# Layer 0 of a two-layer gated attention kernel: tables and mask made in steps 5 to 9, maxima over partitions by turning, first loads in pieces, slots cleared beside attention

## The chip, the core and the metric

The kernel runs on one core of a Trainium2 chip. The metric is the device time in microseconds, the median of several runs. The core has a matrix engine (PE), a vector engine (DVE), an activation engine (ACT), a general engine (POOL) and an engine that mostly issues transfers (SP). Each works through its own queue of instructions in order and waits on semaphores for the others. 16 DMA engines carry the transfers, and all of this kernel's plain transfers but the row scatters are issued from SP's queue.

## The reference, cut to what matters

```python
# x: (4, 512, 512); ctx: (4, 512, 512)
x = x + tanh(g_xattn[0]) * L0_xattn(layernorm(x), ctx)   # fp8-like rounding of both, then x @ ctx^T
x = x + tanh(g_ffn[0])   * L0_ffn(layernorm(x), w1, w2)  # 1.58-bit weights, int8-like rows, gelu twice
x = x + tanh(g_xattn[1]) * L1_xattn(layernorm(x), ctx, ctx, mask, ...)  # 16 heads, ALiBi, softmax
x = x + tanh(g_ffn[1])   * L1_ffn(layernorm(x), ...)     # 8 experts, top 2, plus a shared expert

def quant_dequant_weight_128x128(w):          # used on ctx in L0_xattn
    amax = max(|block of 128 x 128|)          # a maximum over 128 partitions too
    safe = maximum(amax, 1e-6)
    return float(fp8(block * (448 / safe))) * (safe / 448)
```

Layer 0 needs, of the context, one maximum for each block of 128 x 128. Layer 1's attention needs tables (ALiBi slopes and mask rows in bf16) that are added to the scores by small matmuls, and a column form of the mask. Layer 1's experts need a buffer in DRAM, `slots`, that is cleared before rows are scattered into it.

## The kernel before, in words

The 2048 rows of x are 16 tiles of 128 rows; four tiles share one of four context batches. Layer 0 is a software pipeline of steps, `step(s)` for s from -7 to 17. Step s works on several tiles at once: `cross_rows` and `cross_product` for tiles s+7 and s+6 (layer norm, rounding in blocks, product with the context, added to x), `row_stats`, `row_norm`, `row_quant`, `row_ready` for tiles s+1 to s+6 (layer norm, int16 rows, a transpose by DMA, conversion to bf16), `hidden` for tile s (the first feed-forward product and two gelus), `hidden_scales` and `hidden_quant` for tile s-1 (maximum, scale, int16 rows, a transpose by DMA in `turn`), and `down` for tile s-2 (the second product). So the feed-forward of tile 0 begins in step 0; steps -7 to -1 fill the pipeline, and beside them the weights w1 and w2 are loaded, summed (`weight_sum`), averaged (`weight_mean`) and rounded (`weight_round`).

`cross_context(b)` prepares batch b of the context: keys and values for layer 1 by matmuls with wk and wv, the blocks' maxima (line 681 within partitions, line 683 over the partitions by `partition_all_reduce` on POOL), and then, for each of four chunks, a scaling by `up` (line 692), the rounding in four DVE instructions (`fp8_round`, lines 136 to 141) and a scaling back on ACT (line 699).

The program's order is not the engines' order. A recording layer takes all the instructions and a planner places them on each engine by their costs and by what they need; only those given to `keep_in_program_order` (in layer 0 the ACT instructions under `pin`) stay in the order written. The order is fixed when the program is built: at run time each engine goes through its queue in order, and an instruction whose input is late holds up all behind it.

At the start, `load_batch(0)` brings 1024 KB of context in one transfer and `load_rows(0)` 1024 KB of x in one (lines 568 and 572); then come the gates, wk, wv, and the mask's column form, which lines 589 to 604 turn into `mk` and `mbias`. `tables(tmp)` (lines 160 to 219) makes the layer 1 tables: `pick` (line 189, four POOL copies of 128x128), `by_query` (line 191, two POOL copies of 128x2048), and on DVE and ACT the ALiBi rows (lines 197 to 210); line 212 loads the mask's rows and line 217 copies them into `by_key` in four transfers, which wait on SP for DVE. The planner put nearly all of this at the head of the queues.

Eight semaphores are handed round the transfers of SP's queue: a transfer waits until the one eight before it has landed.

`clear_slots` (line 1028) writes zeros from `row_tables`' tail to `slots`, 771 KB for each of 13 transfers; its calls stand in the attention's loop, but it waits for nothing there, and the planner put all 13 on SP between 55 and 104 us.

Attention is a loop over 16 groups, each of four units. For group n the maxima are made in turn n, they are turned and copied into `by_query` rows (line 340) in turn n+1, and the weights are made in turn n+2; `keys` (line 238) fetches a group's keys two turns ahead. Two turns of it stand within the last steps of layer 0. After attention come the shared expert, the router, the scatter into `slots`, and 36 expert tiles.

Of the kernel before, what the change touches and what calls it, by code (L numbers as in the profile page):

```python
# [10 lines left out]
F32 = mybir.dt.float32  # L11
# [37 lines left out]
def flamingo_kernel(  # L49
# [110 lines left out]
    def tables(pool):  # L160

        place_i = pool.tile([P, 1], I32, name="place_i")
# [24 lines left out]
        for b in range(B):  # L187
            nc.vector.tensor_tensor(own[b], own[b], no_mask, ALU.add)
            nc.gpsimd.tensor_copy(pick[:, b, :], own[b].to_broadcast([P, P]))
        for n in range(2):  # L190
            nc.gpsimd.tensor_copy(
                by_query[n], no_mask.unsqueeze(2).to_broadcast([P, NG, S])
            )
# [9 lines left out]
        split3(ali3, ali, ali_rest)  # L203
        nc.vector.tensor_scalar(ali, ali3[:, 0, :], part[0], late, ALU.mult, ALU.add)
# [9 lines left out]
        nc.vector.tensor_scalar(mrow, mrow8, -1.0, 2.0**100, ALU.add, ALU.mult)  # L214
        for i in range(HPG):
# [18 lines left out]
    def keys(b, g):  # L234

        k4 = qk.tile([P, S], F32, tag="k4", name=f"k4_{b}_{g}", bufs=5)
        for i in range(HPG):
            nc.sync.dma_start(
                out=k4[32 * i : 32 * i + 32, :], in_=kT[32 * g : 32 * g + 32, b, :]
            )  # L240
        state["k4", b, g] = k4
# [306 lines left out]
    with ExitStack() as l0:  # L548
# [9 lines left out]
        with ExitStack() as ph:  # L558
# [7 lines left out]
            def load_batch(b):  # L566
                c = cpool.tile([P, DC, S], F32, tag="ctx", name=f"ctx_{b}")
                nc.sync.dma_start(out=c, in_=ctxT[b].rearrange("(c p) n -> p c n", p=P))
                state["ctx", b] = c

            def load_rows(b):
                nc.sync.dma_start(
                    out=x_sb[:, b * TB : (b + 1) * TB, :], in_=x_t[:, b * TB : (b + 1) * TB, :]
                )
# [10 lines left out]


            mk8 = wkv.tile([P, B, TB], U8, name="mk8")
            nc.sync.dma_start(out=mk8, in_=mask_col)
            nc.vector.tensor_copy(mk, mk8)
            cnt_ps = acc("cnt_ps")  # L590
            nc.tensor.matmul(
                cnt_ps[:, : B * TB],
                lhsT=ones,
                rhs=mk.rearrange("p b c -> p (b c)"),
                start=True,
                stop=True,
            )
            anyk = wkv.tile([P, B], F32, name="anyk")
            nc.vector.tensor_reduce(
                anyk, cnt_ps[:, : B * TB].rearrange("p (b c) -> p b c", b=B), AX.X, ALU.max  # L600
            )
            nc.vector.tensor_scalar_min(anyk, anyk, 1.0)
            for b in range(B):
                nc.vector.tensor_scalar(
# [939 lines left out]
```

## Time and profile before

| What | us |
|---|---|
| Runs, median of 3 (lowest to highest) | 1310.45 (1305.22 to 1312.64) |
| The profiled execution: time, span | 1314.13, 1312.4 |
| Feed-forward of tile 0 starts on PE (line 837) | 113.20 |
| Feed-forward of tile 15 starts on PE | 308.53 |
| Attention's first scores on PE | 320.32 |
| First expert tile's transposes on PE | 993.87 |
| PE busy in the span | 1182.9 (90%) |
| DVE, ACT, POOL busy in the span | 609.9, 512.9, 426.1 |

A row of the time line gives the start in us, the time from the first to the last instruction in us, the engine, the line of the code, the operation, what it writes and reads, the count, and in brackets how long the engine sat idle before it and what released it; `issue` there is time in which nothing that the profile shows was waited for. SPq rows are the issuing of transfers, not the transfers. Instructions on DVE overlap a little, so that ten of 0.68 us follow each other every 0.60 us. A row of the windows gives, for a stretch of the span, each engine's busy time (and the number of instructions), then the granted clock of PE as a share of full speed, the DMA engines' busy share, and GB/s.

### The profile page before, as it was taken

How to read it: one execution, taken by the hardware profiler on the slowest of the kernel's cores; microseconds unless marked ns; L12 is line 12 of the kernel's file. 1: busy time of each engine (PE TensorE's matmuls, PEld its weight loads, DVE VectorE, ACT ScalarE, POOL GpSimd, SP SyncE). 2: the span in 40 equal slices, each digit the busy share in tenths (PEclk: the TensorE clock that was granted, in tenths of full speed). 3: DMA queues.
4: the chain of work that ended last, by engine and by line, in shares of the span. 5: the costliest groups of instructions: out<-in, count | busy, mean ns of one | idle time of the engine just before them, and what ended most of it. 6: DMA issues, size and time to landing. Idle time of an engine off the chain costs nothing. (4 is left out here: it accounts for less than half of the span.)

```text
span 1312.4 us, 14470 instructions
## 1 busy us (share of the span) xinstructions
PE 1182.9 (90%) x5348; PEld 546.2 (42%) x5348; DVE 609.9 (46%) x1135; ACT 512.9 (39%) x711; POOL 426.1 (32%) x417
## 2 busy tenths in 40 slices
PE   3457878888799999999999999999999999999995
PEld 2224433333333333333332555543335555555553
DVE  7699887786656666566663501331122111111110
ACT  2588878876255555444454111100001111111111
POOL 3200100010167876776778301126100111111111
PEclk9679988999999999999999899999999999999998
DMA  6782212343000000000003000017315876888782
GB/s 220 259 288 86 45 36 46 92 101 84 17 10 18 9 18 9 10 18 9 2 1 137 9 0 0 0 43 297 87 64 160 265 214 192 255 257 260 220 252 33
DMA packets 88658, 135.33 MB, mean 103 GB/s; under 512 B 52741, under 2 KB 54025, under 8 KB 84745
## 3 DMA queue, kind: packets, MB, share of 16 engines
q1 hardware_dynamic: 80840, 116.52, 27.9%
q0 software_dynamic: 7744, 17.86, 6.3%
q8 instruction: 43, 0.70, 0.2%
q14 instruction: 31, 0.25, 0.1%
HBM read 113.84 MB, written 32.32 MB: 111 GB/s over the span
## 5 line engine op out<-in xcount | busy, mean ns | idle before, releaser
L418 ACT ACTIVATE ex<-s,mbias,mk 128x1024 f32<-128x1024 f32 x128 | 147.2, 1200 | 140.0 <-PE s L232 140.0
L310 DVE TENSOR_REDUCE nmax<-s 128x2 f32<-128x1024 f32 x128 | 150.4, 1216 | 100.6 <-PE s L232 89.8
L1394 PE MATMUL gue<-w,xT 128*128 128x352 f32 x576 | 176.1, 459 | 0.0
L1430 POOL DMA_INDIRECT out_dram<-ye,row_i x36 | 55.7, 1546 | 323.8 <-ACT ye L1429 219.6
L379 POOL TENSOR_TENSOR part<-part,ex 128x1024 f32<-128x1024 f32 x62 | 144.6, 2352 | 16.5 <-PE sm L232 11.4
L1151 PE MATMUL gu<-xnT_d,w 128*128 128x512 f32 x320 | 143.4, 608 | 0.0
L1394 PEld LDWEIGHTS gue<-w,xT 128*128 128x128 f32 x576 | 109.2, 190 | 70.6 <-issue 16.9
L1414 DVE COPY hT<-tph_e 128x256 f32<-128x256 f32 x36 | 15.3, 424 | 255.2 <-PE tph_e L1412 255.2
L1421 PE MATMUL oe<-w,hT 128*128 128x512 f32 (+1 forms) x216 | 102.4, 609 | 3.8 <-ACT ye L1429 0.6
L1151 PEld LDWEIGHTS gu<-xnT_d,w 128*128 128x128 f32 x320 | 62.3, 195 | 77.9 <-issue 77.9
L883 PE MATMUL ob<-w2q,hqT 128*128 128x512 bf16 x256 | 66.1, 412 | 26.1 <-DVE hqT L815 25.4
L1140 ACT ACTIVATE sg<-gu,sgb 128x512 f32<-128x512 f32 x20 | 13.7, 687 | 177.0 <-PE gu L1151 170.8
L379 POOL TENSOR_TENSOR part<-ex,ex 128x1024 f32<-128x1024 f32 x32 | 75.8, 2390 | 21.2 <-ACT ex L418 21.1
L232 PE MATMUL s<-row_tables 10*128 10x512 bf16 (+1 forms) x512 | 68.1, 385 | 13.3 <-DVE nmax L310 10.5
L1402 ACT ACTIVATE sge<-gue 128x352 f32<-128x352 f32 x36 | 16.7, 463 | 151.5 <-PE gue L1394 151.5
L232 PE MATMUL s<-qT,k 32*128 32x512 f32 x512 | 72.4, 605 | 0.0
L232 PE MATMUL s<-k,qT 32*128 32x512 f32 x512 | 72.0, 601 | 0.0
L738 PE MATMUL oa<-ctx,vTa 128*128 128x512 f32 x128 | 63.4, 642 | 8.2 <-ACT vTa L735 8.2
L232 PE MATMUL av<-ex,kv 128*32 128x512 f32 x512 | 69.9, 610 | 0.4 <-ACT ex L418 0.4
L1141 DVE SCALAR_TENSOR_TENSOR hd<-gu,sub,sg 128x512 f32<-128x512 f32 x20 | 15.0, 751 | 117.3 <-ACT sg L1140 104.4
L232 PE MATMUL q_ps<-xnT,wq_sb 128*128 128x512 f32 (+1 forms) x158 | 69.5, 551 | 0.0
L232 PE MATMUL oc<-wo,attnT 128*128 128x512 f32 (+1 forms) x164 | 66.2, 525 | 0.0
(251 smaller groups left out, 1694.2 us busy)
## 6 DMA issues: line engine op xcount, KB each, us to landing
w<-in_e_w_dram SPq DMA_DIRECT2D x36, 1408.0 KB
w<-in_e_w_dram SPq DMA_DIRECT2D x36, 768.0 KB
slots<-row_tables SPq DMA_DIRECT2D x13, 771.0 KB
xr<-slots SPq DMA_DIRECT2D x36, 256.0 KB
ctx<-in_ctxT_dram SPq DMA_DIRECT2D x4, 1024.0 KB
x_sb<-in_x_dram SPq DMA_DIRECT2D x4, 1024.0 KB
stage<-in_w1T_dram SPq DMA_DIRECT2D x4, 1024.0 KB
stage<-in_w2T_dram SPq DMA_DIRECT2D x4, 1024.0 KB
```

Source lines behind the costliest of these rows:

```text
L232: tc.keep_in_program_order(nc.tensor.matmul(*args, **how))
L310: nc.vector.tensor_reduce(nmax[:, i, 2 * j : 2 * j + 2], sc[j], AX.X, ALU.max, negate=True)
L379: nc.gpsimd.tensor_tensor(part[:, hs, :], old[:, hs, :], ex[:, hs, :], ALU.add)
L418: nc.scalar.activation(ex[:, 2 * j : 2 * j + 2, :], sc[j], AF.Exp, bias=mbias[:, b, kc : kc + 1], scale=mk[:, b, kc : kc + 1],)
L738: nc.tensor.matmul(o_ps[:, 0, :], lhsT=vT[:, dc, :], rhs=cq[:, dc, :], start=dc == 0, stop=dc == DC - 1,)
L883: nc.tensor.matmul(o_ps, lhsT=hqT[:, c, :], rhs=w2q[:, c * D : (c + 1) * D], start=c == 0, stop=c == IC - 1,)
L1151: nc.tensor.matmul(gu[:, m, :], lhsT=w[:, dc, c * P : (c + 1) * P], rhs=xnT[:, dc, b * S : (b + 1) * S], start=dc == 0, stop=dc == DC - 1,)
L1394: nc.tensor.matmul(gu[:, m, :I], lhsT=xT[:, dc, :], rhs=wt[:, dc, :], start=dc == 0, stop=dc == DC - 1,)
L1402: nc.scalar.activation(sg, gu[:, 0, :I], AF.Silu)
L1414: nc.vector.tensor_copy(hT[:, :2, :], tp[:, : 2 * P].rearrange("p (c q) -> p c q", q=P))
L1421: nc.tensor.matmul(o_ps[:, 0, :], lhsT=hT[:ni, c, :], rhs=dw[:ni, c, :], start=c == 0, stop=c == len(ICH) - 1,)
L1430: added = nc.gpsimd.indirect_dma_start(out=out, out_offset=bass.IndirectOffsetOnAxis(ap=row_i[:, j, 0:1].bitcast(I32), axis=0), in_=y, in_ ...
```

## The change

- `cross_context`: the maximum over partitions no longer uses POOL. PE transposes the 16 columns of maxima into PSUM (16 x 128), DVE takes the maximum along the row and spreads it over 128 columns, PE transposes that back, and the floor of 1e-6 is taken from PSUM. For batch 0 the maximum within partitions is taken in four pieces of one chunk each.
- `load_batch(0)` and `load_rows(0)` are four transfers each, of 256 KB.
- `tables` is now a generator of five pieces. `pick` and `by_query` are made on DVE from a bf16 tile of ones: four multiplications of 128x128 and eight of 128x512. One piece is made in each of steps 5 to 9, and the mask's column form (now `key_mask`) in step 6. A piece's DVE instructions are queued behind the last maximum of the hidden rows written so far (`state["peak"]`, line 882 of the changed kernel), and its transfers behind the last transpose (`state["turned"]`); its POOL and ACT instructions are free.
- `clear_slots` is queued on SP behind the last key fetch written so far (`state["fetch"]`).

```diff
 def tables(pool):
...
-            nc.gpsimd.tensor_copy(pick[:, b, :], own[b].to_broadcast([P, P]))
+        yield
+        wide = pool.tile([P, S], BF16, name="wide")
+        nc.gpsimd.memset(wide, 1.0)
+        for b in range(B):
+            nc.vector.tensor_scalar_mul(pick[:, b, :], wide[:, :P], own[b])
         for n in range(2):
-            nc.gpsimd.tensor_copy(
-                by_query[n], no_mask.unsqueeze(2).to_broadcast([P, NG, S])
-            )
+            for g in range(NG):
+                nc.vector.tensor_scalar_mul(by_query[n][:, g, :], wide, no_mask)
+        yield
...
 def load_batch(b):
-                nc.sync.dma_start(out=c, in_=ctxT[b].rearrange("(c p) n -> p c n", p=P))
+                src = ctxT[b].rearrange("(c p) n -> p c n", p=P)
+                for dc in [slice(k, k + 1) for k in range(DC)] if b == 0 else [slice(DC)]:
+                    nc.sync.dma_start(out=c[:, dc, :], in_=src[:, dc, :])
...
 def cross_context(b):
-                nc.vector.tensor_reduce(am, cb, AX.X, ALU.max, apply_absolute_value=True)
+                for ns in [slice(4 * dc, 4 * dc + 4) for dc in range(DC)] if b == 0 else [slice(16)]:
+                    nc.vector.tensor_reduce(
+                        am[:, ns], cb[:, ns, :], AX.X, ALU.max, apply_absolute_value=True
+                    )
+                tp = acc(f"tpm_{b}")
+                nc.tensor.transpose(tp[:16, :P], am, ident)
+                peak = small.tile([16, 1], F32, tag="cpeak", name=f"cpeak_{b}", bufs=2)
+                nc.vector.tensor_reduce(peak, tp[:16, :P], AX.X, ALU.max)
+                wide = small.tile([16, P], F32, tag="cwide", name=f"cwide_{b}", bufs=2)
+                nc.vector.tensor_copy(wide, peak.to_broadcast([16, P]))
+                nc.tensor.transpose(tp[:, P : P + 16], wide, ident[:16, :16])
                 safe = small.tile([P, 16], F32, tag="csafe", name=f"csafe_{b}", bufs=2)
-                nc.gpsimd.partition_all_reduce(safe, am, P, bass_isa.ReduceOp.max)
-                nc.vector.tensor_scalar_max(safe, safe, 1e-6)
+                nc.vector.tensor_scalar_max(safe, tp[:, P : P + 16], 1e-6)
...
-                tables(tmp)
                 load_batch(1)
...
-            for s in range(5, NT - 6):
-                step(s)
+            with tc.tile_pool(name="tmp", bufs=1) as tmp:
+                made = tables(tmp)
+
+                def made_here():
+                    with tc.issue_after(state["peak"]), tc.issue_after(state["turned"]):
+                        go(made)
+                        if s == 6:
+                            key_mask()
+
+                for s in range(5, NT - 6):
+                    step(s, [made_here])
...
-                clear_slots(min(3 * (n - 2), MT), min(3 * (n - 2) + 3, MT))
+                with tc.issue_after(state["fetch"]):
+                    clear_slots(min(3 * (n - 2), MT), min(3 * (n - 2) + 3, MT))
```

`load_rows(0)` is cut in the same way as `load_batch(0)`. The order that the planner gives the changed kernel's instructions is known without running it; where the prediction speaks of the new order, it is that. In it POOL's queue holds no `partition_all_reduce`, SP's holds one clearing of `slots` in layer 0 and twelve in attention, and on DVE the pieces of the tables follow the hidden maximum of tile 4.

## The prediction

> **What bounds the kernel now.** I read the slices first, then the windows by stage, then POOL's and DVE's time lines in the first 115 us, then one steady step.
>
> ```profile
> PE   3457878888799999999999999999999999999995
> DVE  7699887786656666566663501331122111111110
> PEclk9679988999999999999999899999999999999998
> ```
>
> Each digit is 32.8 us. From the twelfth on PE is full: attention and the experts are PE's, and whatever starts them earlier ends them earlier. Before that no engine is full all the time, and DVE comes nearest.
>
> ```profile
> 0.00:6.40 6.40, 0.00 (x0) 0.00 (x0) 0.01 (x1) 1.28 (x1) 1.85 (x14) 1.00 0.62 229
> 40.90:46.70 5.80, 0.00 (x0) 0.00 (x0) 0.26 (x3) 1.47 (x6) 0.46 (x2) 0.50 0.89 306
> 63.20:113.20 50.00, 34.95 (x133) 19.45 (x132) 47.06 (x126) 37.94 (x72) 2.96 (x3) 0.86 0.75 261
> 113.20:187.50 74.30, 59.39 (x226) 28.41 (x225) 66.67 (x165) 63.86 (x105) 7.17 (x8) 0.93 0.16 31
> 187.50:245.00 57.50, 46.43 (x177) 21.09 (x176) 43.94 (x107) 48.78 (x71) 4.29 (x6) 0.91 0.24 47
> 320.30:1312.40 992.10, 956.81 (x4487) 437.20 (x4486) 353.98 (x496) 277.76 (x357) 381.74 (x354) 0.98 0.31 95
> ```
>
> Third busy column: DVE works 47.06 of the 50 us ahead of tile 0's feed-forward (113.20) and 66.67 of the next 74.3. So the start is DVE's, but for two holes, the first load and 40.9 to 46.7. In the last row PE works 956.81 of 992.10: 35 us are idle, and no edit but the slot writes touches this stage.
>
> ```profile
> 16.74 4.18 POOL L191 CAST row_tables<-no_mask 128x2048 bf16<-128x2048 f32 x2
> 27.89 8.93 POOL L126 TENSOR_TENSOR rstd_a<-ve_a,mhalf 128x4 f32<-128x4 f32 x1 [6.96 <-DVE ce L136]
> 46.24 0.39 POOL L683 PARTITION_ALL_REDUCE csafe<-cam  x1 [9.42 <-issue]
> 62.75 0.39 POOL L683 PARTITION_ALL_REDUCE csafe<-cam  x1 [6.11 <-issue]
> ```
>
> The same power on 128x4 takes 1.05 us elsewhere and 8.93 here, and each all-reduce that follows a power has an unexplained 6 to 9 us ahead of it: POOL changes over between the two kinds, and each change costs that. DVE pays:
>
> ```profile
> 6.39 2.29 DVE L681 TENSOR_REDUCE cam<-ctx 128x16 f32<-128x2048 f32 x1 [6.39 <-DMA ctx<-in_ctxT_dram]
> 17.23 1.94 DVE L206 SCALAR_TENSOR_TENSOR ali<-ali,part,ali 128x512 f32<-128x512 bf16 x1
> 46.66 0.62 DVE L684 TENSOR_SCALAR csafe<-csafe 128x16 f32<-128x16 f32 x1 [5.54 <-POOL csafe L683]
> 63.17 0.17 DVE L684 TENSOR_SCALAR csafe<-csafe 128x16 f32<-128x16 f32 x1 [3.78 <-POOL csafe L683]
> ```
>
> 5.54 and 3.78 us stand still at the head of DVE's queue. L206 takes 1.94 beside POOL's L191 and 0.84 without it; the csafe at 19.10 takes 1.86 against 0.17.
>
> **The start, part by part.** Removed from DVE ahead of tile 0: the tables and mask. From start to start in the time line between 8.59 and 27.12 they fill 9.2 us, and with the 1.8 us that csafe was held and 0.45 idle at the mask's count, 11.4. Removed waits: 5.54 and 3.78. Earlier data: the context's 1024 KB is issued at 0.81 and read at 6.39, so the DMA engines move it at about 390 GB/s (the slice's rate) after 2.6 us. A quarter is then moved 2 us sooner and the four reductions of 128x512 (0.60 each, row L711) end at 7.0 instead of 8.7. Sum removed: 11.4 + 9.3 + 1.7 = 22.4 us.
>
> Added: in the new order, other waits. I walk it. Statistics of x end at 10.0 (pieces of x land 0.7 apart, four times 0.60 and 0.09). The power on POOL, 1.05 and the way there, lets va start at 11.2. Three normalizations at 0.455, three maxima at 0.60 and 12 small ones at 0.075: 15.3. Context 1's maximum (2.2) and four statistics (2.8): 20.3. The turned maximum of batch 0 waits here. wk is now issued behind the eight pieces, when the third has landed (about 5.8, before 3.18); on PE the key product (6.58) and value product (3.73) stand ahead of the turning, from about 10.5, so to 20.8. The turning itself, the trace has not: two transposes (0.25 each) and two DVE operations on 16 rows, bounded by 0.15 (small ones) and 0.68 (128x512) each. I take 0.2, and 1.5 with the hops: 22.3; the bounds make it 22 to 24. Rounding of context 0, four times 0.60 + 0.34 + 0.34 + 0.60 + 0.60 = 9.9: 32.2. Two rounded rows, 3.2; ACT's turn: va of tile 0 is rescaled from 36 on. Before: 51.95 (L724). **So 16 us earlier.**
>
> From here PE's list is the same as before, and the product of tile 1 is added to x 18 us later in both (before 51.95 to 70.96): at 54.6. DVE has run dry twice by then (3 and 7 us): the new late thing is PE's row product. Ahead of tile 0's feed-forward the new order leaves 38.3 us of DVE work (some 110 instructions at the rows' prices), the power waits add 1.5: its int16 rows are converted at 94.5 to 95.5, and PE is not held as it was by `wmean` behind a 2.2 us maximum (106.9 to 109.07). Start on PE about 97 against 113.2, with equal DVE work left (76.5 us of non-table work done in the new order, 77.4 before). **Gain 16.2.** Bounds: 10, if wk or the hops are late by what the two dry spells cost again (6), and 21, if they vanish by half.
>
> [...] The row: eight issues at 0.45 to 0.5 us each, and 391 to 425 GB/s once transfers of 1024 KB overlap. [...]
>
> **Steps 5 to 9.** Back come 9.2 - 1.1 of tables, 8 by_query products at 0.20 from start to start (nearest row: xqT, 128x512 to bf16, L815) and 4 picks at 0.13: about 10.2, and up to 12.2 if each of the twelve runs as 128x512 f32 (0.34). ACT gets two casts, 0.62 each; POOL almost nothing. A steady step shows the room:
>
> ```profile
> 235.53 0.15 DVE L762 TENSOR_SCALAR nc_h<-hss 128x1 f32<-128x1 f32 x1 [1.14 <-ACT hq L860]
> 236.41 0.21 DVE L864 TENSOR_SCALAR ham<-ham,nc_h 128x1 f32<-128x1 f32 x1 [0.72 <-POOL nc_h L765]
> 237.36 0.69 DVE L815 TENSOR_SCALAR hqT<-hqT 128x2048 bf16<-128x2048 int16 x1 [0.17 <-DMA hqT<-hq]
> 238.11 2.12 PE L883 MATMUL ob<-w2q,hqT 128*128 128x512 bf16 x9 [1.69 <-DVE hqT L815]
> 240.97 2.29 DVE L862 TENSOR_REDUCE ham<-h 128x1 f32<-128x2048 f32 x1 [0.59 <-ACT h L852]
> ```
>
> DVE idles 2.6 us a step, but PE waits for hqT's conversion, and what stands ahead of it on DVE delays the loop. By the new order: tile 4's step, 1.3 us of small ones while DVE waits for ACT anyway (1.81 at 195.8): 0. Next, picks and by_query, 2.1 us: up to 1. Next, two ALiBi lines: 0.5. Next, L151, L210, two L206 and the first by_key line, 3.2 us, less the 1.1 and 0.7 of waiting: 2 to 2.8. Last: 0.3. The casts stand ahead of hq's scaling: 1. Sum 5. Against it, the step from tile 5 to 6 (187.5 to 208.0, 8 us over its neighbours) waits for context 3's rounding (ACT 3.74 behind L141), and the new order finishes that ahead of tile 4's maximum instead of behind it: I credit 1, bound 8. **Loss 4, bounds -3 and 12.2 + 1.2 = 13.4.** On SP, four mask copies (2.91 us of issue) go ahead of one transpose; SP issues two a step of 11 us, 1.7 to 1.8 each, and has room: 0, bound 2.9.
>
> **Slots.** The writes at 55.19 (6 x 771 KB) moved at about 370 GB/s to 69: 2.1 us each. w2's loads and context 3 are then free of them, but ACT did not wait for those loads: 0. In attention each write stands behind a key fetch (420.86 to 423.3), 11 us ahead of the next row copies (434.53), and those have about 12 us until they are used: 0, bound 13 x 2.1 = 27.
>
> **Sum.** 16.2 - 4 = 12.2: the profiled 1314.13 would be 1301.9, and from the median, 3.7 lower, 1298.2. I say 1298.
>
> **The rivals.**
> 1. The tables return in full: DVE and ACT pay 13.4 in steps 5 to 9, as if its 2.6 us a step were not there. For it: the steps to 187.5 leave DVE 10%. Against: half of the pieces stand in waits. 16.2 - 13.4 = 2.8: 1308.
> 2. Slower: attention's row copies are held by the slot writes in the DMA engines, all 13 on the path, 27 us: 1310.4 - 12.2 + 27 = 1325. It decides once a write and the copies behind it take over 12 us, or one is issued right ahead of the copies. Against: DMA is at most a tenth busy there.
> 3. The long step goes too (8) and half of the tables' cost: 16.2 - 2 + 7 = 21: 1289.
>
> **Chances.** A change below 0.5% (6.6 us) can't be told from none. Forecast 0.62 (1292 to 1304), rival 1 0.20 (1304 to 1311), rival 2 0.05, rival 3 0.13. Faster by over 0.5%: 0.62 + 0.13 = 0.75; within 0.20; slower 0.05. From 1288 to 1309 leaves out rival 2, some of 1 and half of 3, under 0.2.
>
> **What would show it.** Start: no powers of 9 us on POOL, csafe from PE at about 22, tile 0's feed-forward at 94 to 100; if at 103 or later, the row product or wk is dearer than walked. Steps: from tile 0's to tile 15's feed-forward 195.3 us before, about 199 after; PE's wait for hqT longer in the step of L151 to L216. Attention to end: 992 us, unchanged; if more, rival 2.

## The result and the profile after

The kernel after takes 1303.49 us, the median of 22 executions (1294.45 to 1310.57), against 1313.71 before, the median of 22 (1305.22 to 1321.65); the 1310.45 known ahead of the prediction is the median of the first three of them. The ratio is 0.9922, 95% interval 0.9903 to 0.9941: the change made the kernel faster by 0.8%, about 10 us, where 1310.45 to 1298 (0.9905) was forecast. The profiled execution of the changed kernel took 1304.45 with a span of 1302.7, the one of before 1314.13 and 1312.4.

The slices of the kernel after, for PE, DVE and PE's granted clock; each digit is 32.6 us:

```profile
PE   3776798887899999999999999998999999999995
DVE  7689999767556665656654401331122111111110
PEclk8878999999899999999999999998999999999998
```

The row of PE reaches 7 in its second digit instead of its fourth. The clock row has its lower digits at other places, which will matter. Now the windows by stage of the kernel after; the columns are those of the prediction's windows, the last three are the granted clock, DMA's share and GB/s:

```profile
23.10:36.75 13.65, 0.00 (x0) 0.00 (x0) 13.65 (x29) 11.69 (x26) 0.14 (x1) 0.52 0.91 337
48.90:98.90 50.00, 37.44 (x121) 19.01 (x121) 41.23 (x121) 38.99 (x68) 2.12 (x2) 0.83 0.31 108
98.90:177.21 78.31, 61.44 (x227) 28.73 (x228) 74.59 (x183) 66.40 (x115) 6.88 (x8) 0.91 0.15 29
305.12:726.26 421.14, 405.31 (x2691) 144.70 (x2691) 254.21 (x273) 194.65 (x212) 272.21 (x266) 0.98 0.14 45
```

In the 50 us ahead of tile 0's feed-forward DVE is busy for 41.23 where it was 47.06: it no longer bounds that stretch alone. The last row, from the first scores to the first gate product of the shared expert, is the one that got longer: in the kernel before it is

```profile
320.32:737.44 417.12, 401.62 (x2692) 144.15 (x2691) 253.81 (x273) 194.67 (x212) 272.16 (x266) 0.99 0.07 21
```

The same 2691 matmuls (one record differs) take 3.7 us more of PE, at 0.98 of the clock in place of 0.99. DVE's head-of-queue waits of 5.54 and 3.78 us at csafe became, in the kernel after (time line of DVE):

```profile
21.53 0.28 DVE L699 TENSOR_REDUCE cpeak<-tpm 16x1 f32<-16x128 f32 x1 [0.90 <-PE tpm L697]
22.38 0.17 DVE L704 TENSOR_SCALAR csafe<-tpm 128x16 f32<-128x16 f32 x1 [0.24 <-PE tpm L702]
...
44.65 0.75 DVE L765 SCALAR_TENSOR_TENSOR x_sb<-oa,tg,x_sb 128x512 f32<-128x512 f32 x1 [1.95 <-PE oa L758]
...
50.48 0.55 DVE L130 TENSOR_SCALAR va<-x_sb,mv_a,rstd_a 128x512 f32<-128x512 f32 x1 [4.13 <-PE tpa L751]
...
54.80 0.75 DVE L765 SCALAR_TENSOR_TENSOR x_sb<-oa,tg,x_sb 128x512 f32<-128x512 f32 x1 [2.30 <-PE oa L758]
...
97.05 0.75 DVE L765 SCALAR_TENSOR_TENSOR x_sb<-oa,tg,x_sb 128x512 f32<-128x512 f32 x1 [2.02 <-PE oa L758]
```

The brackets are the idle time ahead of the row and what ended it: the waits for POOL are gone, and DVE now waits for PE's row products (oa) and for the transposes between them (tpa).

I use six marks in every kernel's trace below. "Tile 0" is the start of tile 0's first product with w1q (h_ps on PE), "0 to 6", "6 to 10" and "10 to 15" the time between such starts, "scores" the first score product of attention, "to gate" the time from there to the first gate product (gu), and "low" the time at half clock in "to gate", in stretches of 3.41 us (explained further down). Each row is one profiled execution, whose own time stands beside the median of its kernel, of 7 to 22 executions; the ratio is to the kernel before beside it on the same chip. One execution lies up to 8.4 us from its median (only_tables, whole_loads and after_again happen to be the shortest of theirs, allreduce_back the longest), so the marks show mechanisms, and only the ratios show times.

| kernel | tile 0 | 0 to 6 | 6 to 10 | 10 to 15 | scores | to gate | low | own time / median | ratio, 95% |
|---|---|---|---|---|---|---|---|---|---|
| before | 113.20 | 94.8 | 48.1 | 52.4 | 320.32 | 417.1 | 2.3 | 1314.13 / 1313.71 | |
| after | 98.90 | 90.2 | 54.6 | 51.3 | 305.12 | 421.1 | 5.0 | 1304.45 / 1303.49 | 0.9922 (0.9903 to 0.9941) |
| after_again | 96.44 | 90.9 | 54.6 | 51.3 | 303.30 | 423.7 | 6.7 | 1303.71 / 1308.00 | 0.9956 (0.9936 to 0.9977) |
| whole_loads | 96.62 | 89.6 | 52.9 | 51.1 | 301.86 | 417.5 | 2.5 | 1292.18 / 1299.64 | 0.9933 (0.9898 to 0.9968) |
| allreduce_back | 106.76 | 94.7 | 52.9 | 51.3 | 315.63 | 419.6 | 4.0 | 1311.95 / 1305.22 | 0.9949 (0.9923 to 0.9974) |
| tables_first | 105.47 | 90.9 | 48.6 | 50.9 | 307.63 | 417.5 | 2.5 | 1299.72 / 1299.13 | 0.9910 (0.9878 to 0.9941) |
| slots_free | 97.84 | 90.1 | 54.4 | 51.3 | 303.68 | 421.2 | 5.0 | 1306.75 / 1301.98 | 0.9921 (0.9890 to 0.9952) |
| only_turning | 106.98 | 88.2 | 50.3 | 51.3 | 306.86 | 421.5 | 5.1 | 1305.29 / 1306.10 | 0.9932 (0.9909 to 0.9956) |
| only_tables | 102.84 | 94.6 | 52.9 | 51.3 | 311.64 | 419.6 | 4.0 | 1302.64 / 1311.04 | 0.9985 (0.9957 to 1.0012) |
| wk_first | 98.06 | 90.0 | 54.4 | 51.3 | 303.88 | 421.1 | 5.0 | 1304.39 / 1306.90 | 0.9930 (0.9902 to 0.9958) |
| warm_start | 98.03 | 89.1 | 54.6 | 52.4 | 304.20 | 420.6 | 4.0 | 1307.24 / 1305.22 | 0.9949 (0.9920 to 0.9977) |
| warm_att | 98.50 | 90.0 | 54.6 | 51.3 | 304.54 | 416.8 | 2.0 | 1300.24 / 1301.70 | 0.9919 (0.9891 to 0.9947) |
| tables_twice | 98.14 | 90.0 | 59.0 | 50.4 | 307.82 | 423.6 | 6.7 | 1314.40 / 1310.19 | 0.9982 (0.9950 to 1.0013) |
| turning_warm | 106.08 | 88.4 | 50.3 | 51.4 | 307.99 | 415.4 | 1.0 | 1304.87 / 1306.20 | 0.9938 (0.9913 to 0.9963) |

In the first two rows the change gains 14.3 us at tile 0 and 15.2 at the scores, and gives 4.0 back in "to gate" and 1.5 behind it (to the end: 575.0 before, 576.5 after): 9.7 in the spans. So two questions stood: which part carries the gain, and what takes 4 us back in a stage that only the slot writes touch.

### The profile page after: what moved, and what is told of

Its sections match the earlier page's. It is cut to its first block, busy times and chain, and to the rows that moved or that the text cites. A ratio compares the mean times of both kernels' runs of the same rounds, so it can differ in the third digit from the quotient of the medians.

```text
span 1302.7 us, 14507 instructions
## 1 busy us (share of the span) xinstructions
PE 1189.5 (91%) x5356; PEld 547.2 (42%) x5356; DVE 609.3 (47%) x1158; ACT 512.6 (39%) x711; POOL 410.9 (32%) x408
## 5 line engine op out<-in xcount | busy, mean ns | idle before, releaser
L387 POOL TENSOR_TENSOR part<-part,ex 128x1024 f32<-128x1024 f32 x62 | 144.6, 2354 | 16.5 <-PE sm L239 11.4
L758 PE MATMUL oa<-ctx,vTa 128*128 128x512 f32 x128 | 67.9, 680 | 18.8 <-ACT vTa L755 18.7
L904 PE MATMUL ob<-w2q,hqT 128*128 128x512 bf16 x256 | 62.7, 397 | 20.3 <-DVE hqT L835 16.5
L239 PE MATMUL s<-row_tables 10*128 10x512 bf16 (+1 forms) x512 | 68.3, 389 | 13.4 <-DVE nmax L318 10.4
L239 PE MATMUL s<-k,qT 32*128 32x512 f32 x512 | 75.2, 625 | 0.0
```

The lines of the kernel that those rows point to most:

```text
L239: tc.keep_in_program_order(nc.tensor.matmul(*args, **how))
L387: nc.gpsimd.tensor_tensor(part[:, hs, :], old[:, hs, :], ex[:, hs, :], ALU.add)
L758: nc.tensor.matmul(o_ps[:, 0, :], lhsT=vT[:, dc, :], rhs=cq[:, dc, :], start=dc == 0, stop=dc == DC - 1,)
L904: nc.tensor.matmul(o_ps, lhsT=hqT[:, c, :], rhs=w2q[:, c * D : (c + 1) * D], start=c == 0, stop=c == IC - 1,)
```

## The experiments

**One part undone at a time.** All four start from the changed kernel.

whole_loads:

```
-for dc in [slice(k, k + 1) for k in range(DC)] if b == 0 else [slice(DC)]:
+for dc in [slice(DC)]:
...
-for ts in [slice(t, t + 1) for t in range(TB)] if b == 0 else [slice(b * TB, b * TB + TB)]:
+for ts in [slice(b * TB, b * TB + TB)]:
...
-for ns in [slice(4 * dc, 4 * dc + 4) for dc in range(DC)] if b == 0 else [slice(16)]:
+for ns in [slice(16)]:
```

> The changed kernel with its first loads whole again (context 0 in one transfer, its four batches of rows in one, one maximum over 2048). What the prediction said: the pieces let the maxima over the context end 1.7 us earlier, so without them the feed-forward of tile 0 starts at 100.6 in place of 98.90 and the whole is 1.7 us longer. Rival: the pieces cost what they give, since their eight issues put the load of wk later (wk and the products of PE behind it end the wait for the turned maximum at 21.5): then without them tile 0 starts between 97 and 99.5. A third view, that the pieces are most of the gain, asks for tile 0 at 104 or later.

Measured: tile 0 at 96.62, on the rival's side and a little beyond it. Up to the first product of tile 0 the pieces do gain a little: x of tile 0 is added to at 44.65 with them and at 45.48 without, 0.8 us. wk is issued at 3.10 here, at 5.52 in the kernel after, but lands at 11.37 against 11.46: the order of the issues hardly moves it. Of the 2.3 us at tile 0, 1.7 come later, from the last row product ahead of it. First the kernel after, then this one (PE's time line):

```profile
91.61 5.40 PE L758 MATMUL oa<-ctx,vTa 128*128 128x512 f32 x8 [0.57 <-ACT vTa L755]
```

```profile
91.03 3.70 PE L758 MATMUL oa<-ctx,vTa 128*128 128x512 f32 x8 [0.56 <-ACT vTa L755]
```

The same eight matmuls: 5.40 us where the granted clock fell to 0.70 from 90 to 95, 3.70 where it didn't. So the pieces are worth under 1 us; most of what differs beyond that is the clock, and the other 0.6 us at 91 was not followed up. The whole, 0.9933, can't be told from the changed kernel's 0.9922. That the first 2 MB come in eight transfers has no price here: in the kernel after they are issued from 0.81 to 4.53, they overlap (291 to 383 GB/s in each microsecond from 2 to 8), and the first is read at 3.46.

allreduce_back (the maxima over partitions on POOL again):

```
-tp = acc(f"tpm_{b}")
-nc.tensor.transpose(tp[:16, :P], am, ident)
...
-nc.vector.tensor_scalar_max(safe, tp[:, P : P + 16], 1e-6)
+nc.gpsimd.partition_all_reduce(safe, am, P, bass_isa.ReduceOp.max)
+nc.vector.tensor_scalar_max(safe, safe, 1e-6)
```

> The changed kernel with the maxima over the partitions back on POOL's all-reduce (csafe from POOL, no turning on PE). Theory: POOL pays 6 to 9 us each time that it changes between the all-reduce and the power, so the power of batch 0 takes about 9 us again and va of tile 0 waits for it, and DVE stands 5 us or more at a csafe; tile 0's feed-forward starts 5 to 11 us later than 98.90, at 104 to 110, and the whole is 5 to 11 us longer. Rival: the stalls came from POOL's copies of the tables and from DVE's full list, which are gone; then the all-reduce costs at most 2 us: tile 0 at 99 to 101.

Measured: tile 0 at 106.76, 7.9 us later, as the theory had it. The whole is 0.9949 against 0.9922 and 0.9956: by the first some 3.5 us longer, less than the 5 to 11 of the theory, and the intervals overlap. POOL's time line of this kernel, then the power in the kernel after:

```profile
9.25 0.39 POOL L697 PARTITION_ALL_REDUCE csafe<-cam  x1 [7.46 <-DVE mv_a L122]
22.14 9.70 POOL L126 TENSOR_TENSOR rstd_a<-ve_a,mhalf 128x4 f32<-128x4 f32 x1 [12.50 <-DVE ctx L706]
38.05 0.39 POOL L697 PARTITION_ALL_REDUCE csafe<-cam  x1 [6.21 <-issue]
53.79 0.39 POOL L697 PARTITION_ALL_REDUCE csafe<-cam  x1 [6.06 <-issue]
```

```profile
10.47 1.05 POOL L126 TENSOR_TENSOR rstd_a<-ve_a,mhalf 128x4 f32<-128x4 f32 x1 [6.20 <-DVE ve_a L124]
```

The power takes 9.70 us behind an all-reduce (1.05 in the kernel after), and the all-reduces behind a power and behind an iota have 6.21 and 6.06 us of nothing ahead of them, with no table copies on POOL and far less on DVE. The rows' normalization waits for that power until 31.87; in the kernel after it starts at 11.56. Only 8.65 of these 20 us are the longer power: it also starts late, at 22.14, though its input is written at 11.38, and why is not known. So each of these three changes from the one kind of work to the other costs 6 to 9 us; what causes that no run here shows. And "0 to 6" returns to 94.7: the step from tile 5 to 6 takes 20.7 us again (180.70 to 201.45), where it takes 11.9 in the kernel after.

tables_first (tables, with POOL's copies, and key mask at the start as in the kernel before):

```
-with tc.tile_pool(name="tmp", bufs=1) as tmp:
-    made = tables(tmp)
...
-    for s in range(5, NT - 6):
-        step(s, [made_here])
+for s in range(5, NT - 6):
+    step(s)
...
+tables(tmp)
 load_batch(1)
```

> The changed kernel with the tables and the key mask made at the start again, as in the kernel before (with POOL's copies), pieces and turning kept. Theory: DVE is what the start waits for, so the 11.4 us of tables return nearly in full: tile 0's feed-forward at 107 to 110 in place of 98.90; its steps from tile 0 to tile 15 are 1 to 4 us shorter than the 196.1 of the changed kernel; the whole 5 to 10 us longer than the changed one. Rival: DVE runs dry by 10 us in the first 55 us of the changed kernel (1.17, 0.90, 1.95, 4.13 and 2.30 us), since PE's row product is late; then the tables fill these holes and tile 0 starts at 99 to 103.

Measured: tile 0 at 105.47, 6.6 later: between theory (107 to 110) and rival (99 to 103), so the holes hide nearly half of the 11.4. "6 to 10" falls from 54.6 to 48.6, and the scores come only 2.5 us later. The whole is not longer at all: 0.9910 against 0.9922 and 0.9956, intervals that overlap. The theory's 5 to 10 us are refuted.

slots_free (slot writes where the scheduler puts them, all 13 issued from 30.1 to 76.8):

```
-with tc.issue_after(state["fetch"]):
-    clear_slots(min(3 * (n - 2), MT), min(3 * (n - 2) + 3, MT))
+clear_slots(min(3 * (n - 2), MT), min(3 * (n - 2) + 3, MT))
```

> The changed kernel with the slot writes left where the scheduler puts them, as in the kernel before (13 writes in the first 70 us, none in attention). Theory: the 4.5 us that the changed kernel loses in the first 100 us of attention come from a lower granted clock at PE (0.73 to 0.76 from 340 to 360), not from the writes; so from the last down product to the first expert nothing is gained for the writes' sake (0 to 1 us), and a difference there goes only with the granted clock; at the start the writes cost at most 1 us (tile 0 at 98.9 to 100). Rival: the writes beside attention hold its row copies or PE, and it wins 4 to 5 us back there: 1299.

Measured: "to gate" 421.2, not a tenth less than with the writes; tile 0 at 97.84. The window of that stage in this kernel:

```profile
303.68:724.85 421.17, 405.30 (x2691) 144.82 (x2691) 254.23 (x273) 194.41 (x212) 271.93 (x266) 0.98 0.08 22
```

22 GB/s in place of 45, the same PE time: the rival is out, the slot writes cost attention nothing.

**The clock.** In steps of a quarter of a microsecond the granted clock has two values only, full and half, and half comes in stretches of 3.41 us or whole multiples of it, on a grid that runs on through a whole execution (its edges lie at 3.2 us plus multiples of 3.41 in the profiled execution of the kernel after, and at 0.9 in the next one). The windows on that grid at the start of attention, kernel after (their edges lie 0.1 us off the grid, hence 0.52 and 0.98):

```profile
337.58:341.00 3.42, 2.15 (x21) 0.94 (x24) 3.32 (x4) 0.60 (x1) 0.99 (x1) 1.00 0.00 0
341.00:344.41 3.41, 3.41 (x12) 0.67 (x9) 2.44 (x3) 0.00 (x0) 1.08 (x5) 0.52 0.00 0
344.41:347.82 3.41, 1.69 (x15) 0.51 (x15) 0.73 (x1) 1.84 (x2) 0.00 (x0) 0.98 0.00 0
347.82:351.24 3.42, 2.72 (x11) 1.22 (x11) 0.59 (x1) 1.74 (x2) 0.00 (x0) 0.52 0.00 0
351.24:354.65 3.41, 3.41 (x12) 1.36 (x15) 1.77 (x2) 0.00 (x0) 0.00 (x0) 0.50 0.00 0
354.65:358.06 3.41, 3.41 (x33) 1.48 (x29) 0.53 (x1) 2.51 (x3) 1.29 (x1) 0.98 0.02 5
```

First busy column: PE. After a window with PE busy for 2.15 of 3.42 us the next has half clock (0.52); after 1.69 of 3.41 too, and the one behind that. No DMA moves here. With one at 324 that makes four low stretches in the first 50 us from the scores on; the kernel before has one (from 340.3), and then none until 657.8.

after_again is the changed kernel itself once more.

> The changed kernel itself once more, beside the kernel before and the next three. If the dips of PE's granted clock fall by chance of their phase against the work, then this execution has the same walk on DVE up to the first row products (csafe of batch 0 at 22.4, va of tile 0 rescaled from 36), but dips at other places: tile 0's feed-forward within 96 to 99.5, first scores within 301 to 306, and from the first scores to the first gate product of the shared expert 417 to 422 us, where the changed kernel took 421.1 and the kernel before 417.1. If the dips belong to the instruction stream, they recur within 1 us of where they were: 421 again.

Measured: tile 0 at 96.44 and no low stretch on the row product at 91; scores at 303.30; "to gate" 423.7, just over the 417 to 422 given, with 6.7 low stretches. With all fourteen executions of the table a line fits: "to gate" is 413.9 us plus 1.46 per low stretch, and every row but warm_start's (0.8 off; it has the same attention code) lies within 0.2 us of it, whether its slot writes are in attention (after, whole_loads, tables_first) or not (before, slots_free, only_turning). 1.46 is a little less than half of 3.41, the estimate for a PE that is busy throughout (products of 1.24 and 1.56 us at full clock take 2.31 and 2.93 at half, see warm_att). So the loss in attention is 2.7 (5.0 less 2.3) stretches more in that one execution, 4 us.

Where the low stretches fall goes by where the grid stands when attention starts. before, whole_loads and tables_first come to their first scores 0.5 to 0.6 us into a stretch; all three have low stretches 20 and 337 us behind that, and take 417.1 to 417.5 us. after, slots_free and wk_first come 1.4 to 1.5 us into one: low at 19, 36, 43 (two) and 343, 421.1 to 421.2 us. after_again, allreduce_back, only_turning, only_tables and tables_twice come 2.0 to 2.1 us into one: two low stretches at 18.5 and two at 42.4 in all five, more later in three of them, 419.6 to 423.7 us. (warm_start, at 2.2, has one stretch in place of the second pair.) So at the same place on the grid the changed kernel's attention code takes what the old one took, and its loss of 4 us in the first trace goes with that place. The kernel before was traced once, at the cheapest place; what it takes at the others stays untested.

warm_att adds two matmuls of zero weights where PE waits for the first exponentials:

```
 for i in range(HPG):
+    for _ in range(2 if (name, own, i) == ("s1_0_2_1", 0, 2) else 0):
+        product(state["q_ps"], lhsT=zeros, rhs=state["xnT", 0][:, 0, :], start=False, stop=False)
     product(
         sc[i // 2][:, i % 2, :],
```

> The changed kernel with two matmuls of zero weights (they add nothing to the sum that they run into) where PE waits 2.25 to 2.42 us for the first exponentials of attention, at 346 to 349. Theory: that wait is what brings two stretches of half clock right behind it (347.75 to 355 in the changed kernel, 3.4 us lost); with PE busy they are gone or one is left, and from the first scores to the first gate product it takes 417 to 419.5 us, where four kernels took 421 to 424 with them and three 417.1 to 417.5 without. Rival: the stretches come from elsewhere (the slot writes, the instruction stream) and stay: 421 to 424, and more by up to 1.8 us for the added work.

Measured: "to gate" 416.8 with 2.0 low stretches. First the kernel after, then this one (PE's time line around the wait; the bracket is the idle time):

```profile
345.72 0.38 PE L239 MATMUL s<-row_tables 7*128 7x512 bf16 x2
348.52 0.61 PE L239 MATMUL s<-row_tables 7*128 7x512 bf16 x2 [2.42 <-ACT ex L426]
348.52 2.31 PE L239 MATMUL s<-k,qT 32*128 32x512 f32 x8
350.76 2.93 PE L239 MATMUL q_ps<-xnT,wq_sb 128*128 128x512 f32 x4
```

```profile
345.34 0.39 PE L241 MATMUL s<-row_tables 7*128 7x512 bf16 x2
345.66 1.98 PE L241 MATMUL q_ps<-xnT,zeros 128*128 128x512 f32 x4
347.97 0.39 PE L241 MATMUL s<-row_tables 7*128 7x512 bf16 x2 [0.33 <-ACT ex L436]
347.98 1.24 PE L241 MATMUL s<-k,qT 32*128 32x512 f32 x8
349.15 1.56 PE L241 MATMUL q_ps<-xnT,wq_sb 128*128 128x512 f32 x4
```

With the hole filled the score product behind it takes 1.24 us in place of 2.31 and the query product 1.56 in place of 2.93. Added work made the stage 4 to 7 us shorter than in the two executions of the changed kernel. This execution comes 2.0 us into a stretch, where the five without the filler all have the two low stretches at 42.4; here they are gone. In the whole no gain shows: 0.9919, against 0.9922 and 0.9956 without.

warm_start does the same at the start: 13 matmuls behind the turned maximum of batch 0, 2 behind the mean of w2.

```
 nc.tensor.transpose(tp[:, P : P + 16], wide, ident[:16, :16])
+if b == 0:
+    warm = big("warm")
+    for k in range(13):
+        pin(nc.tensor.matmul(warm[:, 0, :], lhsT=ones, rhs=x_sb[:, k % TB, :], start=True, stop=True))
...
+if k == 1:
+    warm = big("warm_1")
+    for i in range(2):
+        pin(nc.tensor.matmul(warm[:, 0, :], lhsT=ones, rhs=x_sb[:, i, :], start=True, stop=True))
```

> The changed kernel with matmuls added whose results nobody reads, where PE waits at the start: 13 of 128x512 from csafe of batch 0 on (22.6 to about 35) and 2 behind the mean of w2 (88 to 90). Theory: the granted clock of a stretch of 3.4 us goes to half when PE stood idle for much of the stretch before; with PE busy the products from 36.8 to 44.5 and the row product at 91.6 (5.40 us at the low clock, 3.70 without) run at full clock: no low stretch between 26 and 41 nor between 88 and 100, x of tile 0 added to 1 to 2 us earlier, tile 0's feed-forward at 94 to 96.5 where the two runs of the changed kernel have 98.90 and 96.44. Rival: the low clock has another cause, or the products are not on DVE's path: the low stretches stay, or tile 0 stays within 96.4 to 99.

Measured: the low clock from 23 to 35 is gone, but the filler ended at 33.0, 3.08 us ahead of the next transpose, and a low stretch at 35 to 40 (0.66) stayed. From csafe (21.68) to the second row product's result (53.59) the kernel takes 31.9 us, 32.4 in the kernel after: half a microsecond. The last row product ran into a low stretch anyway (6.57 us), and tile 0 is at 98.03. The mechanism shows in part, the gain doesn't: of the 1 to 2 us expected on x of tile 0, 0.4 came, and csafe itself was 0.7 earlier.

**One part done alone**, from the kernel before.

only_turning (the turning, and nothing else, in the kernel before):

```
-nc.gpsimd.partition_all_reduce(safe, am, P, bass_isa.ReduceOp.max)
-nc.vector.tensor_scalar_max(safe, safe, 1e-6)
+tp = acc(f"tpm_{b}")
+nc.tensor.transpose(tp[:16, :P], am, ident)
...
+nc.vector.tensor_scalar_max(safe, tp[:, P : P + 16], 1e-6)
```

> The kernel before with the maxima over partitions turned, and nothing else of the change. By the prediction's sum the turning is worth the two stalls at csafe, 9.3 us less 2 of hops, and the tables the larger part. After the first experiments (tables back at the start: nothing lost in the end; all-reduce back: 10.5 us lost at the first scores) another theory: the turning alone carries the gain, at the start (tile 0 at 105 to 108 in place of 113.2) and in the step from tile 5 to 6, which falls from 20.5 to 13 or 14 us; first scores at 308 to 311, the whole 8 to 10 us under the kernel before. Rival: it only helps where the tables are gone: 2 to 4 us.

Measured: tile 0 at 106.98, "0 to 6" 88.2, the step from tile 5 to 6 11.8 us, scores at 306.86: 13.5 of the change's 15.2 us. 0.9932 in all, 8.7 us in the medians (1306.10 against 1314.79). The theory formed after the first four runs holds, the rival is out. Why that step shrank stands in DVE's time line, first the kernel before, then this one:

```profile
185.29 2.28 DVE L862 TENSOR_REDUCE ham<-h 128x1 f32<-128x2048 f32 x1
...
189.40 0.68 DVE L141 TENSOR_TENSOR ctx<-ctx,ce 128x512 f32<-128x512 f32 x1
```

```profile
177.40 0.68 DVE L141 TENSOR_TENSOR ctx<-ctx,ce 128x512 f32<-128x512 f32 x1
...
180.37 2.28 DVE L868 TENSOR_REDUCE ham<-h 128x1 f32<-128x2048 f32 x1
```

In the kernel before the last subtraction of context 3's rounding (L141) starts at 189.40, 1.9 us behind tile 5's start (187.46); here at 177.40, 6.0 us ahead of it (183.43). It has changed places with the maximum of tile 4's hidden row (L862, L868) in DVE's queue. No late result of POOL is behind that: in the kernel before the all-reduce of context 3 stands at 109.36, and DVE reads its csafe at 130.49 without a wait.

only_tables (tables and key mask moved, and nothing else, in the kernel before):

```
-tables(tmp)
 load_batch(1)
...
-for s in range(5, NT - 6):
-    step(s)
+with tc.tile_pool(name="tmp", bufs=1) as tmp:
+    made = tables(tmp)
...
+    for s in range(5, NT - 6):
+        step(s, [made_here])
```

> The kernel before with the tables and the key mask moved to steps 5 to 9, and nothing else of the change. By the prediction's sum DVE is free of 11.4 us at the start and pays 4 back: tile 0 at 102 to 104, the whole 7 us shorter. The other theory: POOL's changes between power and all-reduce, and the waits at csafe behind them, set the start in place of the tables, so tile 0 comes at 106 to 109, the step from tile 5 to 6 stays at 20 us, and steps 5 to 9 cost 5 to 6: first scores at 315 to 319, the whole 1 to 5 us shorter.

Measured: tile 0 at 102.84, 10.4 us earlier, as the prediction's sum had it and against the other theory; "0 to 6" as long as before (94.6, with the step from tile 5 to 6 at 20.8), "6 to 10" 4.8 longer, scores 8.7 earlier, of which 2.8 are the clock's (see below). In all 0.9985, not told from no change. Each theory has one half right. Alone, the tables' start is worth its DVE time; with the turning beside it (tables_first against after) it is worth 6.6, since PE's row product is then what DVE waits for.

**Sizes.** wk_first (loads of wk and wv ahead of the rows):

```
 load_batch(0)
+nc.sync.dma_start(out=wk_sb, in_=wk.rearrange("(c p) n -> p c n", p=P))
+nc.sync.dma_start(out=wv_sb, in_=wv.rearrange("(c p) n -> p c n", p=P))
 load_rows(0)
```

> The changed kernel with the loads of wk and wv issued between the context's and the rows' first transfers. Theory: PE's key and value products of batch 0 wait for wk, which lands at 11.4, and stand ahead of the turned maximum; with wk at about 7 csafe of batch 0 comes at 17 to 19 in place of 22.4, and DVE's statistics of batch 1, now behind the rounding, fall into its dry 4 us at 46 to 50: tile 0's feed-forward 1 to 3 us earlier than the changed kernel's in this call. Rival: the rounding only moves ahead of the statistics, DVE does the same work, and x lands later: tile 0 within 1 us, or later.

Measured: the rival. wk is there at 8.23, but the rows' statistics start at 9.63 in place of 6.89, and the second turning starts at 20.73 (22.11 in the kernel after), so that csafe comes at 21, not at 17 to 19: between the two turnings it waits 3.09 us for DVE. x of tile 0 is added to at 45.02 against 44.65: nothing gained.

tables_twice (the heavy pieces made twice):

```
-for b in range(B):
+for b in 2 * list(range(B)):
     nc.vector.tensor_scalar_mul(pick[:, b, :], wide[:, :P], own[b])
-for n in range(2):
+for n in 2 * list(range(2)):
     for g in range(NG):
         nc.vector.tensor_scalar_mul(by_query[n][:, g, :], wide, no_mask)
...
+for _ in range(2):
     nc.vector.tensor_scalar(ali, ali3[:, 0, :], part[0], late, ALU.mult, ALU.add)
     ...
-for g in range(NG):
+for g in 2 * list(range(NG)):
     nc.vector.tensor_scalar(times, late, 1.0 - 4.0**-g, 4.0**-g, ALU.mult, ALU.add)
     nc.vector.tensor_scalar_mul(by_key[:, g, :], ali, times)
```

> The changed kernel with the heavy pieces of the tables made twice over in steps 5 to 8 (picks, by_query, the ALiBi lines and by_key: some 7 us more on DVE, results the same). With the tables at the start steps from tile 0 to 15 took 190.4 us, with them in the steps 196.1: 5.7 us for 11.4 of DVE and ACT work. Theory: DVE's room in these steps is used up by the first time, and what stands ahead of hqT's conversion delays the loop, so the second time costs 4 to 7 us: tile 0 to 15 at 200 to 203. Rival: DVE has 2.6 us of idle a step, and the steps hide the second time as they hid half of the first: 196 to 199.

Measured: from tile 0 to 15 199.3, 3.2 us for some 7: the rival's upper end, just short of the theory's. The cost lies in one place. DVE's time line:

```profile
196.27 2.97 DVE L197 TENSOR_SCALAR row_tables<-wide,no_mask 128x512 bf16<-128x512 bf16 x11
199.16 0.74 DVE L766 SCALAR_TENSOR_TENSOR x_sb<-oa,tg,x_sb 128x512 f32<-128x512 f32 x1
199.82 1.39 DVE L197 TENSOR_SCALAR row_tables<-wide,no_mask 128x512 bf16<-128x512 bf16 x5
201.13 0.16 DVE L600 CAST mk<-mk 128x16 f32<-128x16 uint8 x1
201.21 0.68 DVE L836 TENSOR_SCALAR hqT<-hqT 128x2048 bf16<-128x2048 int16 x1
```

Sixteen writes of by_query stand in a row ahead of the conversion of hqT that PE waits for, and the step from tile 6 to 7 takes 19.7 us in place of 14.1 (two low stretches, from 199.9 on, fall into it too). Next to the other pieces, spread over three steps, the second time is free.

turning_warm (the kernel before with the diffs of only_turning and warm_att):

> The kernel before with two edits: the turned maxima, and the two matmuls of zero weights at attention's first wait for exponentials. The turning alone had first scores at 306.86 and then took 421.5 us to the first gate product, with low stretches between 345 and 355. Theory: the turning carries nearly all of the gain that the change has, and the filler takes off the low clock that eats into it: 417 to 419.5 us from the first scores on, the whole 10 to 14 us under the kernel before, as good as any kernel of this study. Rival: the gain of the filler in the changed kernel was luck of that execution: 421 again, and 7 to 9 us under the kernel before.

Measured: "to gate" 415.4, the shortest of all, with one low stretch; scores at 307.99. That the filler did this is not shown: the execution comes 0.6 us into a stretch, and at that place no kernel has the two low stretches that the filler is to remove. tables_first, at the same place and without a filler, waits as long (PE's time line):

```profile
349.59 0.39 PE L232 MATMUL s<-row_tables 7*128 7x512 bf16 x2 [2.24 <-ACT ex L419]
349.60 1.24 PE L232 MATMUL s<-k,qT 32*128 32x512 f32 x8
```

The score product takes 1.24 us behind a wait of 2.24: full clock. What turning_warm has less of low clock than tables_first is the stretch at 337 us, far behind the filler, and half a one at the stage's end. The whole is 0.9938, 9.6 us in the medians, where 10 to 14 were expected, and no better than only_turning's 0.9932: behind the gate product this execution lost what it had won (579.8 us to the end, with 7.7 low stretches; 575.2 and 6.5 in only_turning, which by the line above explains under 2 of the 4.6 us). So of the kernels run none is shown to beat the changed one: warm_att (0.9919) and tables_first (0.9910) are the lowest, and their intervals overlap with its own.

## Why the prediction was right, point by point

The time came where the range had it, 1303.49 against 1298 (1288 to 1309), and by the path given: an earlier start, less a loss in the steps. Of the 5.5 us between the two, 3.3 are the median before, which rose from 1310.45 to 1313.71 with more executions; the change was sized at 12.2 and measured at 10.2. The shares given to its parts did not hold. The tables are the largest term of the prediction's sum (11.4 of 22.4), and with them back at the start (tables_first, 0.9910) the kernel is no slower; the turning alone brings 13.5 of the 15.2 us at the scores.

- **The start: right.** The walk held to 1 us almost to its end: the context's maxima ended at 6.9 (7.0 said), va started at 11.56 (11.2), csafe came at 22.38 (22.3), the rounding of context 0 ended at 33.0 (32.2), va of tile 0 was rescaled from 36.33 (36), tile 1's product added at 54.80 (54.6; the two rows before that the prediction takes as 18 us apart, 51.95 and 70.96, are 19.0 apart, and 18.5 were measured). Tile 0 came at 98.90, and at 96.44 in a second execution (97): a gain of 14.3 and 16.8 where 16.2 was said. The dry spells on DVE were 6.1 us (1.95 and 4.13) and 2.3 where I had 3 and 7, in the same place and for the cause given, PE's row products and their transposes.
- **What carries it.** Alone, the turning gives 6.2 at tile 0 and the tables 10.4; together 14.3 to 16.8. The pieces give 0.8 at the first product and nothing that can be seen later; the 1.7 of the sum was too much, since wk, which PE waits for, lands at 11.4 either way.
- **Steps 5 to 9: the sum failed in its credit, not in its cost.** I priced the tables at 5 in these steps; "6 to 10" shows 4.8 (only_tables) and 6.0 (after against tables_first). But I credited 1, with a bound of 8, for the step from tile 5 to 6. It shrank by 8.6 (20.5 to 11.9), wherever the turning was in; the steps ahead of it grew by 4.0, so that "0 to 6" gained 4.6. Loss from tile 0 to 15: 0.8 in place of 4, and 1.9 without the 1.1 that the clock gave back. The mechanism was the one named, context 3's rounding ending ahead of tile 5 instead of behind it; what I did not see is that it belongs to the turning, not to the room on DVE. Why the scheduler orders DVE's work otherwise with the turning is not known.
- **Slots: right at 0.** Rival 2 asked for more than 992 us from the scores to the end, and 997.6 were measured. Its mark was met and its mechanism was not: slots_free has the same 421 without a write. The mark was a bad one, because it did not leave out the clock.
- **What the sum did not have: the clock.** With more half clock than before, the kernel lost 4.0 us in "to gate" (and 1.5 behind it, not traced to a cause); and 2.8 us of the gain ahead of it are also the clock's: the change puts no work on PE, DVE or ACT between tile 10 and the scores, and yet these stretches went from 52.4 and 11.8 to 51.3 and 10.1 (the kernel before had two more low stretches, from 285.7 and 316.4). Without those 2.8 the change won 12.4 us to the scores (15.2 less 2.8), against 12.2 in the prediction's sum. That these agree so closely is luck: the start fell 1.9 short of its 16.2, the steps lost 1.9 in place of 4, and the second execution of the same kernel gained 17.0 at the scores. The prediction compared a span to a span as if both had the same clock.
- **Rival 1** (all 13.4 back) is out: 4.8 to 6.0. **Rival 3** (the long step goes too) was half right: it did, by 8.6, but 4.0 of it went into the steps ahead.

What stays open: the parts' shares of the time itself. The turning alone has 0.9932, all but the turning 0.9949, the tables alone 0.9985, all but the tables 0.9910; the first two intervals overlap widely, and the first and the third only just don't. That the turning carries the larger part rests on the marks and on two kernels, not on a difference of times.

## What to carry to other kernels

A part that frees an engine at the start is worth what the next late thing leaves of it: walk the new order to the next wait, here PE's row product behind DVE, instead of adding up what goes. An all-reduce on POOL between powers or iotas cost 6 to 9 us here at each change from the one kind of work to the other that no other wait hid. The largest single step that taking it out saved (8.6 us) stood over a hundred microseconds behind the first of them, in the order that the scheduler gave DVE's queue: compare the queues' orders too, not only the waits. And before a few microseconds in a stage that the change doesn't touch are put down to the change, count the stretches of low clock in both traces, and see where the grid stood when the stage began.

## What the runs showed of the hardware that was not expected

PE's granted clock was full or half in whole stretches of 3.41 us, on a grid whose phase differed between executions (an edge at 2.4 us in the kernel before, 3.2 in the kernel after, 0.9 in after_again). In the fourteen executions, from PE's first work on, half clock followed every stretch with PE busy for less than 0.40 of it; the lowest share that full clock followed was 0.52 in the kernel before (stretch from 118.5 us) and 0.43 in the kernel after (from 132.9). Above 0.40 the busy share does not decide. 0.50 and 0.63 in the fence of the kernel after were followed by half clock, 0.54 in tables_first (348.02 to 351.43, behind its wait of 2.24 us) by full, and a stretch that is busy throughout, but with transposes and products of eight columns, by half again (kernel after, windows):

```profile
723.42:726.84 3.42, 3.42 (x30) 3.18 (x29) 1.77 (x6) 2.46 (x3) 0.00 (x0) 1.00 0.00 0
726.84:730.25 3.41, 3.41 (x6) 1.33 (x5) 2.40 (x7) 0.00 (x0) 0.80 (x2) 0.50 0.00 0
```

Why half clock followed there no run shows. It also followed single waits of 1.5 and 2.4 us (1.51 ahead of 646.80 and 2.42 ahead of 348.52 in the kernel after), though not each such wait. The same wait of 1.5 us (DVE's maximum, at 645.3 in the kernel after and 641.8 in warm_att) brought a low stretch in the one and none in the other:

```profile
646.80 0.39 PE L239 MATMUL s<-row_tables 10*128 10x512 bf16 x2 [1.51 <-DVE nmax L318]
646.81 1.24 PE L239 MATMUL s<-qT,k 32*128 32x512 f32 x8
647.98 1.64 PE L239 MATMUL av<-ex,kv 128*32 128x512 f32 x8
```

```profile
643.28 0.39 PE L241 MATMUL s<-row_tables 10*128 10x512 bf16 x2 [1.52 <-DVE nmax L328]
643.29 1.24 PE L241 MATMUL s<-qT,k 32*128 32x512 f32 x8
644.46 1.06 PE L241 MATMUL av<-ex,kv 128*32 128x512 f32 x8
```

The product with ex takes 1.64 us in the first and 1.06 in the second. In both the wait lies wholly in one stretch, with PE busy for 1.90 of its 3.41 us; what decides between them stays open. The low stretches go with the larger part of the scatter between executions of one kernel: 22 of the changed one lie between 1294.45 (mean granted clock 0.970) and 1310.57 (0.961), and their times follow their clocks with a correlation of -0.85.
